# The tail behind an attention stream: gate, strip order, moved modes, transform places and last store, changed together

## The chip, the cores and the metric

The kernel runs on one core of one Trainium2 chip. The time is device time of one execution in microseconds (us), the median of the runs. A core has TensorE (PE: matmuls, with weight loads PEld beside them), VectorE (DVE), ScalarE (ACT), GpSimd (POOL) and SyncE (SP); each works through its own instructions in order, and they wait for one another by semaphores. SP, ACT and POOL issue DMA transfers, and all transfers of the core are moved by its 16 DMA engines. SBUF is the working memory with 128 partitions; PSUM is the memory that TensorE writes, eight banks of 2 KB a partition (512 fp32 numbers).

## The reference

Everything is fp32. The input x has shape (4, 64, 96, 96). Two layers follow one another, each applied to a group-normalised input (32 groups of two channels) and added to its own input:

```python
x = x + L0(gn(x))
x = x + L1(gn(x))
```

Layer 0 is attention over the N = 9216 pixels with a sigmoid in place of a softmax, and a channel gate:

```python
q, k, v = conv1x1(x, wq) + bq, conv1x1(x, wk) + bk, conv1x1(x, wv) + bv  # 8, 8 and 64 channels
out = V @ sigmoid(Q^T K)^T + x                                           # per image, 9216 x 9216
avg, mx = out.mean((2, 3)), out.max((2, 3))
mlp = lambda f: relu(f @ ca_w1.T) @ ca_w2.T
result = out * sigmoid(mlp(avg) + mlp(mx))[:, :, None, None]
```

Layer 1 is a spectral convolution. A real 2-D Fourier transform is taken of each channel; only 16 modes along w and 32 along h (the first and the last 16) are kept; for each mode the 64 input channels are mixed into 64 output channels by a complex matrix; the other modes are zero, and the transform back gives the result.

## The kernel before, in words

**Layout.** An image lies in SBUF as 128 partitions by 4608 columns: channel by half of the image (`x1`, `xs[p]`). A strip is 768 columns (8 rows in each half), six to an image. A block is 512 columns of queries, nine to an image.

**The stream.** For four images, one after another, TensorE computes energies (line 551), ScalarE takes the sigmoid from PSUM to SBUF (572), and TensorE multiplies by the values and accumulates over all keys in one bank (589). At the end of each block VectorE adds the bank to the block and sums it (595) and takes its maximum (597). The order of TensorE, ScalarE and VectorE is written out by hand here (`manual_schedule`, lists of steps `together`, `alone`, `ends` by time step `t`); the layer-1 work of images 0 to 2 is worked in among it. Only the last image's second layer is left when the stream ends; that is the tail, from line 914.

**Gate.** `after(p)` (612) makes three steps. `means` reduces the nine maxima and nine sums of the blocks and joins the halves; `hidden` is two small products (629, 630) and two steps on VectorE (631, 632); `gates` is one product with two columns (636), a sum of the two (639) and a sigmoid (640). Ahead of these, three matmuls without a use (917, 918) are queued on TensorE behind the last attention product.

**Strips.** The last image becomes x1 = x * gate + old x. The old x has been read again into `again` during the stream. For strips not in `ADDED`, VectorE does this (`combine`, 177); for those in `ADDED`, ScalarE scales (990) and GpSimd issues a DMA that adds `again` to x1 in SBUF (991). `strip(s)` (993) then transposes the strip on VectorE (997) into a place `t0` to `t3`, squares and sums it on ScalarE (1002) and multiplies it on TensorE by the transform along w (1007); three strips go into each of two groups. Steps of the normalisation (`group_stats`, 134) come between. Each group is turned (1014) and multiplied along h (1019), the result is turned again (1049) and scaled into `u` (1051, 1054). This part is again in a hand-written order for TensorE, ScalarE and VectorE; the rest of the tail is ordered by the compiler's scheduler. Weights of the modes are loaded into whatever room has come free (936): four rows once the stream ends, then into the strips' places and into `again`.

**Modes.** Eight steps q, each with two halves, mix four rows of modes with four matmul groups (215); the results go by turns through VectorE (130) and ScalarE (132) into `vms[q]`. They must change partitions for the transform back. For q up to 5, `keep` (224) stores them to DRAM (`vd`) in four DMAs and `back` (229) reads them in another order into `vt`: rows 0 to 15 by four DMAs of GpSimd behind q = 4, rows 16 to 23 by four of SP behind q = 5. For q = 6 and 7 TensorE moves them with selecting matrices into the PSUM tile `picked` (1096). Line 1100 adds `picked` to `vt`.

**Transform back and stores.** Two groups of products along h (1111) go into two PSUM tiles of two banks, four transposes (1117) into `z`. For each of six strips TensorE makes `py` (1127), in one of two PSUM places of two banks, VectorE adds it to x1 (1135) and a DMA stores it (`write`, 97), by turns from SP and ScalarE. Strip 0 goes in two halves.

`occupy` (961) queues matmuls without a use behind a given one.

## Time and profile before

| what | us |
|---|---|
| median of 3 runs (lowest, highest) | 3021.2 (3020.45, 3021.38) |
| profiled execution, whole | 3020.43 |
| its span, first to last instruction | 3018.7 |
| matmuls without a use begin behind the stream (918) | 2962.3 |
| gate (640) | 2965.8 |
| first transpose of a strip (997) | 2967.1 |
| mode products begin (215) | 2984.1 |
| add of moved modes (1100) | 3001.8 |
| first add of a last strip (1135) | 3007.2 |
| last add of a last strip begins (1135) | 3012.9 |
| TensorE busy | 3000.9 |
| ScalarE busy | 2406.6 |
| VectorE busy | 335.8 |

Times in the span count from its first instruction. A row of the timeline gives start, length, engine, line, operation, what it writes and reads, and in brackets how long the engine was idle before it and what the profile takes to have ended this. A row with x3 holds several instructions of the same kind, whose length then includes gaps. fp32 matmuls appear as two instructions each. "DMA to landing" is counted from an issue to the arrival of all its data. Where a wait is for several semaphores, the profile names one of them.

### The profile page before, as it was taken

The numbers are of one execution on the slowest core, as the hardware profiler recorded it, in microseconds if no ns is written. First come the engines' busy times: TensorE is split into PE (matmuls) and PEld (weight loads), VectorE is DVE, ScalarE is ACT, GpSimd is POOL, SyncE is SP. The second block draws the span as 40 slices with busy tenths as digits, with TensorE's granted clock in tenths as the row PEclk, the third lists the DMA queues.
The fourth block names the chain that finished last, engine by engine and source line by source line (L and its number), as shares of the span: only waits on it lengthen the run. The fifth ranks groups of instructions, "written<-read, shape, count | busy, mean of one in ns | idle before, by whom it ended". The sixth has DMA issues, their size and how long they took to land.

```text
span 3018.7 us, 44581 instructions
## 1 busy us (share of the span) xinstructions
PE 3000.9 (99%) x19360; PEld 1091.3 (36%) x19360; DVE 335.8 (11%) x814; ACT 2406.6 (80%) x1539; POOL 145.0 (5%) x295
## 2 busy tenths in 40 slices
PE   9999999999999999999999999999999999999998
PEld 3333333333333333333333333333333333333334
DVE  4100000002111000001311000000221110100104
ACT  5888888887887888888788888888788777777783
POOL 1100000004000000001300000000310000000000
PEclk9999999999999999999999999999999999999999
DMA  4000000002230000001322000000243243312224
GB/s 167 20 4 4 4 4 4 4 2 56 68 77 17 4 4 4 4 5 23 82 69 72 4 4 4 4 3 2 44 109 98 77 158 86 55 47 64 67 93 153
DMA packets 157267, 133.96 MB, mean 44 GB/s; under 512 B 118960, under 2 KB 123120, under 8 KB 156784
## 3 DMA queue, kind: packets, MB, share of 16 engines
q1 hardware_dynamic: 145152, 110.06, 13.5%
q0 software_dynamic: 11344, 19.69, 2.2%
q8 instruction: 152, 2.49, 0.3%
q10 hardware_dynamic: 576, 1.38, 0.1%
q14 instruction: 43, 0.35, 0.0%
HBM read 91.53 MB, written 38.73 MB: 43 GB/s over the span
## 4 chain that ended last, share of the span: by engine, by line
PE 98%; DVE 1%; DMA 0%; ACT 0%; issue 0%; SPq 0%; POOL 0%; DVEq 0%; ACTq 0%
PE banks L589 78%; PE banks L551 17%; PE banks L470 1%; PE banks L215 1%; PE banks L394 0%; PE pv L215 0%; PE banks L300 0%; PE banks L366 0%; DMA x<-in_x_dram 0%; PE banks L328 0%; ACT at L572 0%; PE pa L1007 0%; DVE xt L997 0%; PE banks L436 0%; DVE x L180 0%
## 5 line engine op out<-in xcount | busy, mean ns | idle before, releaser
L572 ACT ACTIVATE at<-banks 128x2048 f32<-128x2048 f32 (+1 forms) x1505 | 2388.9, 1638 | 548.2 <-PE banks L551 535.8
L589 PE MATMUL banks<-at,vT 128*64 128x512 f32 (+1 forms) x11780 | 2406.6, 548 | 0.0
L589 PEld LDWEIGHTS banks<-at,vT 128*64 128x64 f32 x11780 | 773.8, 136 | 1352.3 <-issue 1297.5
L551 PE MATMUL banks<-q,kT 32*128 32x512 f32 x5040 | 543.0, 452 | 0.3 <-ACT at L572 0.3
L551 PEld LDWEIGHTS banks<-q,kT 32*128 32x128 f32 x5040 | 223.6, 182 | 453.0 <-issue 331.4
L595 DVE SCALAR_TENSOR_TENSOR x<-banks,x 128x512 f32<-128x512 f32 x36 | 24.9, 692 | 1663.4 <-PE banks L589 1663.4
L521 POOL DMA_DIRECT2D stage<-qk x256 | 125.7, 499 | 937.7 <-DMA qk<-turned 927.1
L168 POOL TENSOR_TENSOR mr_l<-ve_l,cs 128x1 f32<-128x1 f32 x7 | 3.9, 556 | 1288.7 <-DVE ve_l L167 1288.7
L398 DVE TENSOR_TENSOR x<-banks,x 128x768 f32<-128x768 f32 x18 | 17.2, 958 | 212.3 <-PE banks L394 212.3
L470 PEld LDWEIGHTS banks<-cs,x 64*64 64x64 f32 x1152 | 22.6, 135 | 27.2 <-ACT at L572 25.6
L487 DVE TENSOR_TENSOR u<-banks,cs 128x128 f32<-128x128 f32 x35 | 10.2, 291 | 191.0 <-PE banks L470 191.0
L739 POOL DMA_DIRECT2D w_early<-in_spec_dram x12 | 6.4, 542 | 518.5 <-PE banks L394 357.7
L470 PE MATMUL banks<-cs,x 64*64 64x80 f32 (+1 forms) x1152 | 28.3, 236 | 0.0
L477 DVE TENSOR_TENSOR vT<-banks,cs 128x256 f32<-128x256 f32 x72 | 26.9, 415 | 0.0
L715 DVE COPY ae<-banks 128x512 f32<-128x512 f32 x9 | 6.2, 692 | 174.8 <-PE banks L300 128.8
L597 DVE TENSOR_REDUCE maxs<-x 128x1 f32<-128x512 f32 x36 | 24.7, 686 | 1.2
L715 DVE COPY ws<-banks 128x512 f32<-128x512 f32 x16 | 11.1, 692 | 116.8 <-PE banks L215 116.8
L603 DVE BATCH_NORM_STATS2 stats<-x 128x6 f32<-128x512 f32 x36 | 23.3, 681 | 4.3 <-DMA x<-in_x_dram 4.3
L180 DVE SCALAR_TENSOR_TENSOR x<-x,gate,old 128x768 f32<-128x768 f32 x18 | 18.2, 1009 | 17.5 <-DMA old<-in_x_dram 17.5
L508 DVE STREAM_TRANSPOSE turned<-t 128x384 f32<-128x384 f32 (+1 forms) x35 | 19.9, 568 | 1.4 <-DVE t L506 0.3
L551 PE MATMUL banks<-q_first,kT 32*128 32x512 f32 x144 | 16.6, 463 | 2.7 <-ACT at L572 1.8
L523 DVE CAST kT<-stage 128x256 fp32r<-128x256 f32 x64 | 16.0, 287 | 24.3 <-DMA stage<-qk 24.1
(144 smaller groups left out, 402.0 us busy)
## 6 DMA issues: line engine op xcount, KB each, us to landing
ws<-in_spec_dram SPq DMA_DIRECT2D x32, 512.0 KB
q<-qk SPq DMA_DIRECT2D x280, 32.0 KB
stage<-qk POOLq DMA_DIRECT2D x256, 32.0 KB, 1.9
out_dram<-x SPq DMA_DIRECT2D x20, 384.0 KB
x<-in_x_dram SPq DMA_DIRECT2D x9, 768.0 KB
old<-in_x_dram SPq DMA_DIRECT2D x18, 384.0 KB
x1d<-x SPq DMA_DIRECT2D x18, 384.0 KB
xd<-old SPq DMA_DIRECT2D x18, 384.0 KB
```

The costliest lines, as they stand in the source:

```text
L180: nc.vector.scalar_tensor_tensor(xs[p][:, cols], xs[p][:, cols], gate, old, ALU.mult, ALU.add)
L215: self.last = nc.tensor.matmul(pv[bass.ts(g, 32), :].rearrange("q (n k o) -> q n k o", n=SIDE, o=C)[:, :, k, :], self.ut[:, at:at + 32], s ...
L470: projected[0] = nc.tensor.matmul(pp[bass.ts(e, P // 2), b, 2 * a + h, :width], src[rows, a, h, bass.ts(e, P // 2)], named("wv")[rows, :wi ...
L477: nc.vector.tensor_tensor(vTs[p % 2][:, 8 * s:8 * s + 8, :].rearrange("p (a h b) m -> p b a h m", h=2, b=2)[:, b], pp[:, b, :, :C].rearran ...
L508: nc.vector.transpose(turned[:, k:].rearrange("p k a (m h) -> p (k a) h m", h=2), t[:, k:].rearrange("p k a h m -> p (k a) h m").bitcast(F32))
L521: nc.gpsimd.dma_start(come[bass.ts(r, QK), :], split[p][s // 2][:, r // 2, bass.ts(s % 2, NB // 2)])
L551: nc.tensor.matmul(banks[:, bank_of(i), :], kT[r:r + 32, i % TILES // 8, i // 4 % 2, :], ask[i // TILES][r:r + 32, :], start=True, stop=True)
L572: nc.scalar.activation(at[:, of:of + n, :], banks[:, bank:bank + n, :], AF.Sigmoid)
L589: attended[0] = nc.tensor.matmul(acc[half, cols], vTs[n // NBLK % 2][:, j, :], at[:, place(2 * pair + b), cols], start=(j == 0), stop=(j = ...
L595: nc.vector.scalar_tensor_tensor(blk, acc, 1.0, blk, ALU.mult, ALU.add, accum_out=sums[p][:, m:m + 1])
L597: mark[0] = nc.vector.tensor_reduce(maxs[p][:, m:m + 1], blk, AX.X, ALU.max)
L603: each = [lambda s=s: nc.vector.bn_stats(stats[:, s, :], xs[p][:, bass.ts(s, NB)]) for s in range(NBLK)]
```

## The change

Seven edits, all of the last image's tail or its preparation:

- `after_last` takes the place of `after` for the last image. Three sums and a maximum over what is known before the last block are taken in the last block of the stream (`known`). At the end of the last block, ScalarE sums the accumulator bank while writing it to a scratch place, and VectorE adds the bank to the block and takes the maximum in one instruction, starting from the known maximum. `means` has three steps in place of five, `hidden` one in place of two ahead of the next product, and the two columns are summed by accumulating in PSUM; the sigmoid reads PSUM.
- Strips go in the order 0, 1, 3, 2, 4, 5, and `ADDED` is (2, 5) in place of (4, 5). Places and steps between go by the position in this order.
- The stores of q = 5 are shared between SP and ScalarE; of the four reads of rows 16 to 23, SP issues two, GpSimd one, and ScalarE one, behind q = 7.
- `picked` has two banks, and its products are ordered by q first.
- The add of `picked` to `vt` is split in two halves of output channels.
- The two tiles of the transform along h and those of `py` share four places of two banks.
- The last strip's product, add and store go in two halves, as the first strip's do.

```diff
@@ -65,7 +65,8 @@
 SQ = 32
 NSQ = H // SQ
 NSTRIP = HALF // STRIP
-ADDED = (4, 5)
+ADDED = (2, 5)
+INTURN = (0, 1, 3, 2, 4, 5)
 APART, APART_LAST = 6, 4
 GN_EPS = 1e-5
 
@@ -221,9 +222,9 @@
             vm = self.vms[q].rearrange("q (n m) -> q n m", n=SIDE)
             self.move(vm[:, :, bass.ts(half, 2 * C)], pv.rearrange("q (n m) -> q n m", n=SIDE))
 
-        def keep(self, q, queue):
+        def keep(self, q, *queues):
             for g in range(4):
-                queue.dma_start(self.vd[4 * q + g],
+                queues[g % len(queues)].dma_start(self.vd[4 * q + g],
                                 self.vms[q][32 * g:32 * g + SIDE * 2 * self.n, :])
 
         def back(self, vt, to, first, rows, b, slot, n, parts, queue):
@@ -592,6 +593,13 @@
                 if j == NCH - 1 and cols.stop == NB:
                     p, m = divmod(n, NBLK)
                     blk = xs[p][:, bass.ts(m, NB)]
+                    if n + 1 == B * NBLK:
+                        nc.scalar.activation(at[:, 0, :], acc, AF.Identity,
+                                             accum_out=sums[p][:, m:m + 1])
+                        nc.vector.tensor_tensor_reduce(
+                            blk, acc, blk, 1.0, maxs[p][:, m - 1:m], ALU.add, ALU.max,
+                            accum_out=maxs[p][:, m:m + 1])
+                        continue
                     nc.vector.scalar_tensor_tensor(blk, acc, 1.0, blk, ALU.mult, ALU.add,
                                                    accum_out=sums[p][:, m:m + 1])
                     mark[0] = nc.vector.tensor_reduce(maxs[p][:, m:m + 1], blk, AX.X, ALU.max)
@@ -640,6 +648,48 @@
                 nc.scalar.activation(gate, gsum, AF.Sigmoid)
 
             return gate, [means, hidden, gates], f
+
+        def after_last(p):
+
+
+            f = small.tile([P, 2], F32, tag=f"f{p}", bufs=1, name=f"f_{p}")
+            fm = small.tile([P, 1], F32, tag="tot", name=f"fm_{p}")
+            top = small.tile([C, 1], F32, tag=f"top{p}", bufs=1, name=f"top_{p}")
+            hid = small.tile([R, 2], F32, tag=f"hid{p}", bufs=1, name=f"hid_{p}")
+            gate = small.tile([P, 1], F32, tag=f"gate{p}", bufs=1, name=f"gate_{p}")
+            last = NBLK - 1
+
+            def known():
+                rest = small.tile([P, 2], F32, tag="rest", bufs=1, name=f"rest_{p}")
+                nc.vector.tensor_reduce(rest[:, 0:1], sums[p][:, :last], AX.X, ALU.add)
+                nc.vector.tensor_reduce(rest[:, 1:2], xs[p][:, bass.ts(last, NB)], AX.X, ALU.add)
+                nc.vector.tensor_reduce(maxs[p][:, last - 1:last], maxs[p][:, :last], AX.X, ALU.max)
+                nc.vector.tensor_tensor(rest[:, 0:1], rest[:, 0:1], rest[:, 1:2], ALU.add)
+                known_sum.append(rest[:, 0:1])
+
+            known_sum = []
+
+            def means():
+                nc.vector.tensor_copy(top, maxs[p][C:, last:])
+                nc.vector.tensor_tensor(f[:C, 1:2], maxs[p][:C, last:], top, ALU.max)
+                nc.vector.tensor_scalar(fm, sums[p][:, last:], known_sum[0], 0.5 / HALF,
+                                        ALU.add, ALU.mult)
+
+            def hidden():
+                ph = bank_a(f"ph_{p}")
+                nc.tensor.matmul(ph[:R, 1:2], named("w1", C), f[:C, 1:2], start=True, stop=True)
+                nc.tensor.matmul(ph[:R, 0:1], named("w1"), fm, start=True, stop=True)
+                nc.vector.tensor_scalar(hid, ph[:R, 0:2], 0.0, None, ALU.max)
+                nc.vector.tensor_scalar(f[:, 0:1], fm, 2.0, None, ALU.mult)
+
+            def gates():
+                pg = bank_a(f"pg_{p}")
+                for i in range(2):
+                    projected[0] = nc.tensor.matmul(pg[:, 0:1], named("w2", R), hid[:, i:i + 1],
+                                                    start=(i == 0), stop=(i == 1))
+                nc.scalar.activation(gate, pg[:, 0:1], AF.Sigmoid)
+
+            return gate, [means, hidden, gates], f, known
 
         def warm(s, n=NB // 2):
 
@@ -779,6 +829,7 @@
             follow(None, lambda: fetch(1), 4)
 
         stats0 = {p: stats_of(p) for p in range(1, B)}
+        final = after_last(B - 1)
         ask, asked, known, valued, normal, renewed = {0: q}, 1, 3, 1, 2, NBLK
         heads = [HEAD]
         sizes, total, order, done, block, edges = [5], [5], [[4, 5, 6, 3, 2]], [], [], set()
@@ -818,6 +869,8 @@
                 if p == B and 3 <= m < 6:
                     for s in (2 * m - 6, 2 * m - 5):
                         end(t + 2, lambda s=s: bring(s))
+                if p == B and m == NBLK - 1:
+                    end(t + 2, final[3])
                 if m == NBLK:
                     assert not chain, (n, t, len(chain))
                     second_layer(p - 1, t)
@@ -912,7 +965,7 @@
                         step()
                     put_off = []
         spare[0] = 7
-        gate, steps, f = after(B - 1)
+        gate, steps, f, _ = final
         with tc.issue_after(attended[0].ins):
             for n in (NB, NB, NB // 4):
                 nc.tensor.matmul(banks[:, 3, :n], cs[:, :P], cs[:, :n], start=True, stop=True)
@@ -993,7 +1046,7 @@
         def strip(s):
 
             cols = bass.ts(s, STRIP)
-            xt = place_of(f"t{s % 4}", f"xt_{s}")[:, :STRIP]
+            xt = place_of(f"t{INTURN.index(s) % 4}", f"xt_{s}")[:, :STRIP]
             nc.vector.transpose(xt, x1[:, cols])
             if s == 0:
                 nc.vector.scalar_tensor_tensor(mv[:, 0:1], f[:, 0:1], gate, stats0[p][2][:, 0:1],
@@ -1029,12 +1082,12 @@
         less_constant = small.tile([P, 1], F32, tag="const", name="less_constant")
 
         with tc.manual_schedule(engines=ENGINES):
-            for s in range(NSTRIP):
+            for i, s in enumerate(INTURN):
                 if s not in ADDED:
                     combine(p, s, gate, again[:, bass.ts(s, STRIP)])
                 strip(s)
-                if s in (1, 3):
-                    steps[s // 2]()
+                if i in (1, 3):
+                    steps[i // 2]()
             var = small.tile([P, 1], F32, tag="var", name="var")
             rows_turned(0)
             rows(0)
@@ -1075,36 +1128,45 @@
         for q in range(KH // 4):
             l1.mix(q, 0)
             l1.mix(q, 1)
-            if q <= last - NPICK:
+            if q < last - NPICK:
                 l1.keep(q, nc.sync)
+            if q == last - NPICK:
+                l1.keep(q, nc.sync, nc.scalar)
             if q == 3:
                 nc.gpsimd.memset(vt, 0.0)
-            for first, rows_of, behind, queue in ((0, 16, last - 3, nc.gpsimd),
-                                                  (16, 16 - 4 * NPICK, last - 2, nc.sync)):
+            for first, rows_of, behind, queues in (
+                    (0, 16, last - 3, [nc.gpsimd] * 4),
+                    (16, 16 - 4 * NPICK, last - 2, [nc.sync, nc.gpsimd, nc.sync, None]),
+                    (16, 16 - 4 * NPICK, last, [None, None, None, nc.scalar])):
                 if q == behind:
-                    for half in range(2):
-                        for slot in range(2):
-                            l1.back(vt, 64 * half + 32 * slot, first, rows_of, 0, slot,
-                                    2 * half, 2, queue)
-
-        picked = mix_bank.tile([P, NB], F32, tag="picked", bufs=1, name="picked")
+                    for i, queue in enumerate(queues):
+                        if queue is not None:
+                            l1.back(vt, 64 * (i // 2) + 32 * (i % 2), first, rows_of, 0, i % 2,
+                                    2 * (i // 2), 2, queue)
+
         M = KW // SIDE * C
-        for n in range(2):
-            for q in range(last - NPICK + 1, last + 1):
+        picked = mix_bank.tile([P, 2, NB], F32, tag="picked", bufs=1, name="picked")
+        for q in range(last - NPICK + 1, last + 1):
+            for n in range(2):
                 for half in range(2):
                     at = 4 * (last - q)
                     l1.last = nc.tensor.matmul(
-                        picked[bass.ts(half, C), bass.ts(n, M)],
+                        picked[bass.ts(half, C), n, :M],
                         picks[:, 2 * half + n, at:at + C], l1.vms[q][:, bass.ts(2 * half + n, M)],
                         start=(q == last - NPICK + 1), stop=(q == last))
-        nc.vector.tensor_tensor(vt, picked, vt, ALU.add)
+        for i in range(2):
+            to = vt.rearrange("q (n k o) -> q n k o", n=2, o=C)[..., bass.ts(i, C // 2)]
+            nc.vector.tensor_tensor(
+                to, picked[:, :, :M].rearrange("q n (k o) -> q n k o", o=C)[..., bass.ts(i, C // 2)],
+                to, ALU.add)
         occupy(1, l1.last, mix_bank.tile([P, NB], F32, tag="v", name="idle_v", bufs=6))
 
         banks.close()
-        pz_bank, py_bank = psum("ps_z"), psum("ps_y", 2)
+        y_bank = psum("ps_y", 4)
         z = tail.tile([P, C, SQ], F32, tag="z", name="z_last")
         for i in range(2):
-            pz = pz_bank.tile([P, 4, NB // 2], F32, tag=f"z{i}", name=f"pz_{i}")
+            pz = y_bank.tile([P, 2, NB], F32, tag="y", name=f"pz_{i}")
+            pz = pz.rearrange("q b (x m) -> q (b x) m", m=NB // 2)
             for e in range(2):
                 for half in range(2):
                     rows_of = bass.ts(half, 2 * KH)
@@ -1116,10 +1178,10 @@
                 cols = slice(i * C // 2 + n * C // 4, i * C // 2 + (n + 1) * C // 4)
                 nc.vector.transpose(z[:, cols, :], pz.rearrange(
                     "q x (k o) -> q o (x k)", o=C // 2)[:, bass.ts(n, C // 4), :])
-        occupy(2, moved[0], py_bank.tile([P, 2, NB], F32, tag="y", name="idle_y")[:, 0])
+        occupy(2, moved[0], y_bank.tile([P, 2, NB], F32, tag="y", name="idle_y")[:, 0])
         for s in range(NSTRIP):
-            for part in ([0], [1]) if s == 0 else ([0, 1],):
-                py = py_bank.tile([P, 2, NB], F32, tag="y", name=f"py_{s}_{part[0]}")
+            for part in ([0], [1]) if s in (0, NSTRIP - 1) else ([0, 1],):
+                py = y_bank.tile([P, 2, NB], F32, tag="y", name=f"py_{s}_{part[0]}")
                 for n, i in enumerate(part):
                     for r in range(2):
                         rows_of = bass.ts(r, C)
```

## The prediction

> **What bounds the kernel.** I read the page's chain first, then the table by stretches, then the timeline from 2962 us on, engine by engine. The chain and the two stretches (columns: length, then busy us and instruction count of TensorE, its weight loads, VectorE, ScalarE, GpSimd; clock; DMA share; GB/s):

> ```profile
> PE 98%; DVE 1%; DMA 0%; ACT 0%; issue 0%; SPq 0%; POOL 0%; DVEq 0%; ACTq 0%
> ...
> 0.00:2962.40 2962.40, 2955.03 (x18899) 1061.58 (x18899) 303.17 (x755) 2392.75 (x1514) 139.94 (x286) 1.00 0.15 41
> 2962.40:3018.70 56.30, 45.88 (x462) 29.73 (x462) 32.66 (x59) 13.86 (x25) 5.11 (x9) 0.97 0.64 205
> ```

> TensorE's attention stream holds 2962.4 us at full clock and is untouched, but for four VectorE instructions placed in its last block, where VectorE idles for 76.8 us before the row at line 595; they need some 0.15 + 0.69 + 0.16 + 0.15 us and delay nobody. So only the last 56.3 us can move, and there the order of waits decides, not a busy engine. All times below are on the clock of the span before. The sum is made against the profiled execution: span 3018.7 and 1.7 around it, 3020.4; the median of the runs, 3021.2, lies 0.8 above that, and I carry the difference over to the median.

> **Gate.** The handover from stream to tail (timeline: start, length, engine, line):

> ```profile
> 2962.32 2.21 PE L918 MATMUL banks<-cs 128*128 128x512 f32 x6
> ...
> 2962.44 0.69 DVE L595 SCALAR_TENSOR_TENSOR x<-banks,x 128x512 f32<-128x512 f32 x1 [76.76 <-PE banks L589]
> ...
> 2963.17 0.69 DVE L597 TENSOR_REDUCE maxs<-x 128x1 f32<-128x512 f32 x1
> ...
> 2964.33 0.15 DVE L624 TENSOR_TENSOR f<-f,top 64x1 f32<-64x1 f32 x1
> ...
> 2964.54 0.19 PE L629 MATMUL banks<-f,cs 64*4 64x1 f32 x2
> ...
> 2965.22 0.38 PE L636 MATMUL banks<-hid,cs 4*128 4x2 f32 x2 [0.38 <-DVE hid L632]
> 2965.64 0.16 DVE L639 TENSOR_REDUCE gsum<-banks 128x1 f32<-128x2 f32 x1 [0.47 <-PE banks L636]
> 2965.83 0.20 ACT L640 ACTIVATE gate<-gsum 128x1 f32<-128x1 f32 x1 [6.76 <-DVE gsum L639]
> ```

> The add (0.69) and the maximum (0.69) become a sum on ScalarE beside one fused add-and-maximum on VectorE. The nearest row for the first is the Identity of 128x512 at line 454, 0.69, plus an accumulator read of 0.19 that overlaps it by 0.1; no table load appears between that Identity and the sigmoids, so none is priced. The fused instruction has no row; its floor is line 595's 0.69 + 0.08, its ceiling both passes, 1.38; I take 0.77, as line 595 also reads the bank, adds, writes and accumulates. If both ran at once, VectorE would be through at 2963.2, and three small steps at the spacing of 0.11 to 0.18 would give f at 2963.65, 0.83 earlier than 2964.48. [...] Both read the accumulator's bank. No run here shows two engines on one bank. [...] It makes little odds: the fillers of line 918 sit ahead of the first gate product on TensorE and their last pass starts at about 2964.33 and lasts 0.11, so TensorE is free at 2964.44 either way. Gain there: 0.1. The two hidden steps become one: 0.07 off. The sum of the two columns moves into TensorE: a second pair of passes costs 0.12 (the spacing of lines 629 and 630) to 0.3 (weight loads of 0.18 each); I take 0.25, since the weights are 128 columns here; the reduction saves 0.16 + 0.03. Gate in sum: -0.1 - 0.07 + 0.25 - 0.19 = **-0.1** (ends -0.25 and +0.6, the latter if the fused instruction takes 1.38).

> **Strips.** Before, strips 4 and 5 got their old x by an accumulating DMA; now 2 and 5 do, in the order 0, 1, 3, 2, 4, 5. Counts stay: four combines, six transposes, two scalings.

> ```profile
> DMA to landing us min/median/max: 5.4/6.3/7.2
> ...
> 2967.31 1.79 POOL L991 DMA_DIRECT2D x<-again  x2 [76.39 <-DVE x L180]
> ...
> 2972.17 0.97 DVE L180 SCALAR_TENSOR_TENSOR x<-x,gate,again 128x768 f32<-128x768 f32 x1
> ...
> 2973.18 0.98 DVE L997 STREAM_TRANSPOSE xt<-x 128x768 f32<-128x768 f32 x1
> ...
> 2974.21 4.15 PE L1007 MATMUL pa<-xt,lc 128*128 128x256 f32 x18 [0.35 <-DVE mr_l_last L157]
> ...
> 2974.31 1.98 DVE L997 STREAM_TRANSPOSE xt<-x 128x768 f32<-128x768 f32 x2
> ```

> The first transfer, issued at 2967.31, lands 5.4 later, 2972.7; the second, issued at about 2968.1, 7.2 later, 2975.3. Before, the first was wanted at 2974.3, 1.6 after its landing. Now strip 3's transpose ends at 2972.24 and strip 2's follows at once; it finds its data at 2972.7 and VectorE, in order, waits 0.45. An earlier gate hardly helps, because until about 2969.5 the transfer shares the engines with the four 512 KB loads that the end of the stream releases (DMA share 0.90 to 1.1 from 2967 to 2974). What is queued behind: the mean's two steps, strip 4's combine and transpose, strip 5's transpose. Strip 2 is transposed by 2973.7, strip 4 by 2976.0, strip 5 by 2977.0, where before 5 ended at 2976.3. TensorE needs 1.38 a strip (4.15 / 3): strip 4 from 2976.1, strip 5 from 2977.45 to 2978.85, against 2978.36 before. Without the wait it would be 2978.35: the new order alone gains nothing, as TensorE's last strips follow VectorE. Everything to the mode products (2984.1 before) moves by +0.5, less the gate's 0.1: **+0.4**. Ends: -0.2 (no wait) and +1.0 (landing 0.6 later). Weight loads that wait for strip 2's square start some 2 us later; the last of the loads are in by 2986.5 or so and these rows are used from 2994.5, so 8 us cover them.

> **Moved modes.** Order: store of q = 5 to DRAM, read back, add.

> ```profile
> 2993.63 3.01 SPq L226 DMA_DIRECT2D vd<-w_early  x8
> ...
> 2995.85 2.10 POOL L237 DMA_DIRECT2D vt<-vd  x4 [9.25 <-DMA vd<-w_early]
> ...
> 2998.07 2.28 PE L1096 MATMUL picked<-w_early,lc 128*64 128x256 f32 x16
> 2998.20 0.59 ACT L132 COPY w_early<-pv 128x512 f32<-128x512 f32 x1 [1.14 <-PE pv L215]
> ...
> 2998.82 1.30 SPq L237 DMA_DIRECT2D vt<-vd  x4
> ...
> 3001.81 0.69 DVE L1100 TENSOR_TENSOR vt<-picked,vt 128x512 f32<-128x512 f32 x1 [3.75 <-PE idle_v L965]
> ```

> The wait of line 1100 names TensorE, but the picks end by 3000.4; what came last is the fourth read back, issued at 2999.8, in by 3001.8 (2.0). The stores of q = 5 go out at 2995.35 in four issues of 0.3 and the last, of 2996.3, is in at 2998.75 (2.4). With two on SP and two on ScalarE's queue the last issue is at 2995.7 and all are in at 2998.1. ScalarE pays 2 x 0.34 in a gap of 1.13 before its copy at 2996.47: covered, with 0.45 to spare. Reads back: SP's two are issued by 2998.45, in at 3000.5; GpSimd's fifth waits 2998.1, starts some 0.5 later (its first four started 0.65 after their last wait passed) and lands 2.2 on, 3000.8; ScalarE's goes after its last copy, 2998.82 + 2.0 = 3000.85. The picks, now ordered by q, wait less for that copy and end near 3000. Add at 3000.9: -0.9 (ends -0.2, if one of the other queues is as late as SP was, and -1.2). The add is in halves of about 0.41 (the 128x256 row of line 477), so the first transform can start at 3001.3 where it started at 3002.55: **-1.2** in all. That needs the halves, interleaved in memory, to be told apart; the two engines writing u interleaved at 2982.8 at the same time show that this is done. If not, -0.8.

> **Last transforms and stores.**

> ```profile
> 3007.25 1.02 DVE L1135 TENSOR_TENSOR x<-py,x 128x384 f32<-128x384 f32 x2 [0.84 <-PE py L1127]
> ...
> 3008.86 1.82 DVE L1135 TENSOR_TENSOR x<-py,x 128x768 f32<-128x768 f32 x2 [0.59 <-PE py L1127]
> ```

> With two places the product of strip 1 waits for the first half's add, hence the 0.59. With four it starts 0.35 sooner, and the later waits of 0.19 go: strip 1's add ends 2.2 after the first add's start, not 2.57. From there stores bind: at 3011 to 3015 DMA is at 0.96 to 1.04 of its share with 364 to 393 GB/s, 1.03 us a strip, so five strips take 5.2 whatever VectorE does. So **-0.4**; the halved last store costs 2 x 0.55 - 0.95 = 0.15 on VectorE, which is ahead of the stores by then, and saves nothing while they are backed up. Ends 0 and -0.8.

> **Sum.** +0.4 - 1.2 - 0.4 = -1.2, gate included: span 3017.5, profiled time 3019.2, median **3020.0 us**.

> **Rivals.** (1) My own: strip 2 waits about 0.5, the rest gains; 3020.0, chance 0.50. (2) Strip 2 comes in time: -0.2 - 1.2 - 0.5 = -1.9, up to -2.4 with the larger ends; about 3019.0. For it: the issue may profit from the gate; against it: the shared DMA engines. 0.25. (3) The moved modes gain nothing, the wait only changing queue to GpSimd or ScalarE: +0.4 - 0.3 (the halved add alone) - 0.4 = -0.3, so 3020.9. For it: GpSimd's 0.65 before an issue and its landings of up to 2.6. 0.15. (4) Slower: strip 2 lands with strip 5, at 2975.3, because the two accumulating transfers and the weight load issued at 2970.4 share the DMA engines packet by packet. VectorE then waits 3.1, the mode products move by +3.0, and the end by 3.0 - 1.6 = +1.4: 3022.6. It decides from a landing of about 2973.9, 1.2 after the one shown. Against it: before, the first landed 2.6 ahead of the second. 0.10.

> **Range.** The lowest ends give -2.4 and the runs' scatter 0.5: 3018.2. Above, rival 3 with a wait of 1.0 gives +0.3 and scatter 0.5, 3022.0; this leaves part of rival 4 and the extremes out. Rivals 1 to 3 end on one side, so the one range serves. 0.2% of this time, about what a measurement of this kernel can tell from no change, is 6.0 us: no case reaches it. Same 0.95; 0.02 for faster and 0.03 for slower are left for what no row shows, such as a clock loss in the tail (the clock is 1.00 in every us up to 3015).

> **What would show it.** Right: the add of line 1100's successor starting 0.9 earlier relative to the mode products, the last adds without gaps over 0.2, strip 2's transpose waiting on its DMA, gate within 0.25 of before. Wrong: ScalarE and VectorE on the accumulator together; strip 2 without a wait; the stores ending more than 0.6 earlier after the first add; any change before 2962.

## The result, and the profile after

The changed kernel takes 3024.47 us (median of 20 runs, 3023.28 to 3026.64) where the kernel before takes 3020.43 beside it: 1.0013 times as long, 95% interval 1.0007 to 1.0019. That is within the 0.2% that the forecast called no change, but it is 4.0 us longer where 1.2 us less was predicted, and outside the range. The profiled execution has a span of 3023.5, 4.8 more than before.

First the page's chain, then the two stretches (columns as in the prediction):

```profile
PE 95%; issue 3%; DMA 1%; DVE 0%; ACT 0%; POOL 0%; SPq 0%; DVEq 0%; POOLq 0%; ACTq 0%
```

```profile
0.00:2962.40 2962.40, 2955.31 (x18898) 1061.12 (x18898) 303.71 (x759) 2392.56 (x1514) 140.12 (x286) 1.00 0.14 41
2962.40:3023.50 61.10, 47.60 (x466) 32.02 (x464) 31.78 (x57) 14.52 (x27) 5.66 (x10) 0.93 0.60 189
```

The stream is as before. The tail is 61.1 long instead of 56.3, its mean clock is 0.93 instead of 0.97, and TensorE is busy 1.7 longer in it although it has hardly more to do. The time at which the tail begins scatters between executions, from 2960.7 to 2964.2 in the profiles of this study, so from here on each stage is measured inside the tail. The table has them for all kernels. "Tail" runs from the first of the matmuls without a use (918 before) to the last instruction; "gate" to the start of the sigmoid; "strips" on to the first mode product; "modes" on to the first add of `picked` to `vt`; "back" on to the first add of a last strip; "adds" is the length of these adds; "end" is from the first of them to the last instruction. Spans are given to 0.1 us, so "end" and "tail" are good to 0.05. Each row is one profiled execution. e6 and e10 are one kernel profiled twice, and differ by 0.1 in the strips and by 0.7 in the end.

| kernel | gate | strips | modes | back | adds | end | tail |
|---|---|---|---|---|---|---|---|
| before | 3.51 | 18.29 | 17.69 | 5.44 | 6.60 | 11.45 | 56.38 |
| after | 3.45 | 18.64 | 20.90 | 7.90 | 5.46 | 10.20 | 61.09 |
| e1 | 3.45 | 18.53 | 17.48 | 5.17 | 5.45 | 10.14 | 54.77 |
| e3 | 3.52 | 18.29 | 21.12 | 8.24 | 6.60 | 11.40 | 62.57 |
| e4 | 3.45 | 19.18 | 20.90 | 5.17 | 5.45 | 10.25 | 58.95 |
| e5 | 3.45 | 18.44 | 17.34 | 5.18 | 5.45 | 10.18 | 54.59 |
| e6 | 3.44 | 18.26 | 17.44 | 5.17 | 5.46 | 10.82 | 55.13 |
| e7 | 3.45 | 18.57 | 17.38 | 5.17 | 5.39 | 10.64 | 55.21 |
| e8 | 3.45 | 18.73 | 17.35 | 5.18 | 6.74 | 11.48 | 56.19 |
| e9 | 3.45 | 18.86 | 17.06 | 5.17 | 5.46 | 10.60 | 55.14 |
| e10 | 3.45 | 18.35 | 17.46 | 5.18 | 5.45 | 10.11 | 54.55 |
| e11 | 3.51 | 18.30 | 17.92 | 5.17 | 5.45 | 10.95 | 55.85 |

After less before: gate -0.06, strips +0.35, modes +3.21, back +2.46, end -1.25; in sum +4.7. So two stages lose 5.7, and the rest gains 1.0. Both losing stages have a mark of their own in the profile.

**The modes: SyncE stands still.** SP's own waits, 2985 to 3006 us, in the kernel after (what is waited for, total us, times, longest):

```profile
SPq L227 <- DMA vd<-w_early: 5.0, 1, 5.0
SPq L227 <- DVE vm L131: 3.6, 1, 3.6
SPq L227 <- ACT vm L133: 1.7, 4, 0.7
SPq L238 <- DMA vd<-w_early: 1.4, 5, 0.4
```

and in the kernel before:

```profile
SPq L226 <- DVE vm L130: 3.6, 1, 3.6
SPq L226 <- ACT vm L132: 1.7, 4, 0.7
SPq L237 <- DMA vd<-w_early: 1.6, 3, 0.7
SPq L226 <- ACT w_early L132: 0.6, 2, 0.3
```

The first line after has no counterpart before. In `keep` (line 227), whose DMAs only wait for the copies that fill `vms[q]`, SP waits 5.0 us for another store, one of q = 5. The timelines say which (SP's in the kernel before, then those of SP, ScalarE and GpSimd in the kernel after):

```profile
2986.74 6.46 SPq L226 DMA_DIRECT2D vd<-vm  x16
```

```profile
2987.11 11.39 SPq L227 DMA_DIRECT2D vd<-vm  x16
2998.67 2.06 SPq L227 DMA_DIRECT2D vd<-w_early  x6
3002.51 0.61 SPq L238 DMA_DIRECT2D vt<-vd  x2
```

```profile
2995.75 0.86 ACTq L227 DMA_DIRECT2D vd<-w_early  x2
```

```profile
3001.05 2.68 POOL L238 DMA_DIRECT2D vt<-vd  x5 [14.08 <-DMA vd<-w_early]
```

The sixteen stores of q = 0 to 3 took SP 6.46 us before and take 11.39 now. SP's second store of q = 3 goes out at 2997.56, when ScalarE's first store of q = 5, issued at 2995.75, is done. The chain in order of time names that store, 1.80 from its issue to its landing, and shows what it drags along (start, length, engine, line):

```profile
2995.75 1.80 DMA vd<-w_early
...
2997.56 0.26 SPq L227
...
2999.32 1.74 DMA vd<-w_early
3001.05 1.38 POOL vt L238 x3
...
3003.17 1.96 DMA vt<-vd
...
3005.40 0.44 DVE vt L1159
3005.84 0.04 issue
3005.88 3.96 PE pz L1173 x16
3009.84 2.85 PE idle_y L1018 x4
3012.70 0.58 PE py L1189 x8
```

Behind the waiting store stand two more of q = 3, four of q = 4 and SP's two of q = 5; GpSimd's reads need the last store of q = 4 and start at 3001.05, where they started at 2995.85; the add starts at 3005.40, where it started at 3001.81.

**The way back: the clock.** TensorE before (two rows) and after (four rows; start, length, in brackets the idle time), and then the clock after in stretches (the last three columns are granted clock, DMA share, GB/s):

```profile
3002.55 2.17 PE L1111 MATMUL pz<-vt,lc 64*128 64x256 f32 x16 [1.14 <-DVE vt L1100]
3004.66 1.99 PE L965 MATMUL idle_y<-cs 128*128 128x512 f32 x4
```

```profile
3000.33 1.13 PE L1018 MATMUL idle_v<-cs 128*128 128x512 f32 x2
3005.88 3.96 PE L1173 MATMUL pz<-vt,lc 64*128 64x256 f32 x16 [4.43 <-DVE vt L1159]
3009.77 2.92 PE L1018 MATMUL idle_y<-cs 128*128 128x512 f32 x4
3012.63 4.18 PE L1189 MATMUL py<-lc,z_last 64*64 64x192 f32 x96
```

```profile
3002.00:3004.00 2.00, 0.00 (x0) 0.00 (x0) 0.00 (x0) 0.00 (x0) 1.72 (x4) 1.00 0.30 79
3004.80:3005.00 0.20, 0.00 (x0) 0.00 (x0) 0.00 (x0) 0.00 (x0) 0.00 (x0) 0.68 0.00 0
3006.00:3008.00 2.00, 2.00 (x10) 2.00 (x12) 0.16 (x1) 0.00 (x0) 0.00 (x0) 0.50 0.00 0
3011.60:3011.80 0.20, 0.20 (x2) 0.16 (x1) 0.00 (x0) 0.00 (x0) 0.00 (x0) 0.76 0.00 0
3012.00:3014.00 2.00, 2.00 (x34) 1.38 (x36) 0.70 (x2) 0.00 (x0) 0.00 (x0) 1.00 0.00 0
```

TensorE has nothing to do from 3001.46 to 3005.88. At 3004.87 (0.68 of full speed in that fifth of a us is 36% of it at 1.00 and the rest at 0.50) the granted clock falls to one half, and it is full again at 3011.70. The products along h therefore take 3.96 where they take 2.17 at full clock (the first row, and that of e4 below), and the fillers `idle_y` 2.92 where they take 1.98 (e4): 2.73 together. `py` waits in TensorE's queue behind these fillers, so this all ends on the way to the end.

### The profile page after: what moved, and what is told of

The parts are those of the page before. It is cut to its first block, busy times and chain, and to the rows that moved or that the text cites. A ratio compares the mean times of both kernels' runs of the same rounds, so it can differ in the third digit from the quotient of the medians.

```text
span 3023.5 us, 44602 instructions
## 1 busy us (share of the span) xinstructions
PE 3002.9 (99%) x19362; PEld 1093.1 (36%) x19362; DVE 335.5 (11%) x816; ACT 2407.1 (80%) x1541; POOL 145.8 (5%) x296
## 4 chain that ended last, share of the span: by engine, by line
PE 95%; issue 3%; DMA 1%; DVE 0%; ACT 0%; POOL 0%; SPq 0%; DVEq 0%; POOLq 0%; ACTq 0%
PE banks L590 75%; PE banks L552 16%; PE banks L471 1%; PE banks L216 1%; PE banks L395 0%; PE pv L216 0%; PE banks L301 0%; DMA w_early<-in_spec_dram 0%; PE banks L697 0%; PE banks L367 0%; PE banks L329 0%; DMA x<-again 0%; DVE x L1197 0%; DMA x<-in_x_dram 0%; ACT at L573 0%
## 5 line engine op out<-in xcount | busy, mean ns | idle before, releaser
L488 DVE TENSOR_TENSOR u<-banks,cs 128x128 f32<-128x128 f32 x35 | 10.2, 290 | 191.8 <-PE banks L471 191.8
```

## The experiments

The theory was: a store of ScalarE holds back SP, the add comes some 3 us late, and the clock falls because of the idle time. The first rival was that the reads over three queues, the order of `picked` or the strips' order delay the add. A second was that the loss in the way back is the four shared PSUM places, with the clock only a sign of it.

**e3: the kernel before, with two of the four stores of q = 5 on ScalarE's queue and no other part of the change** (`keep` takes several queues, as in the change).

```diff
...
-            if q <= last - NPICK:
+            if q < last - NPICK:
                 l1.keep(q, nc.sync)
+            if q == last - NPICK:
+                l1.keep(q, nc.sync, nc.scalar)
```

> The kernel before with one edit: two of the four stores of q = 5 go from ScalarE's queue. Theory A: SP stands for some 5 us in its stores of q = 3, the add of the picked modes starts near 3005.2 in place of 3001.8, TensorE idles over 4 us and its clock falls to a half for some us; time near 3026, 6 over before. Theory B: about +1. Theory C: no change, or 0.5 less than before.

Measured: 3026.81 (13 runs), 1.0019 times before, 1.0011 to 1.0027. Modes +3.43, back +2.80, all else as before: this one edit loses 6.4 us. SP's waits and TensorE's row:

```profile
SPq L226 <- DMA vd<-w_early: 5.0, 1, 5.0
```

```profile
3006.30 3.96 PE L1113 MATMUL pz<-vt,lc 64*128 64x256 f32 x16 [4.57 <-DVE vt L1102]
```

Here the two PSUM places of before are in use, and the clock falls all the same. So the reads, the strips and the four places are not needed for the loss.

**e1: the change, with the four stores of q = 5 on SP again.**

```diff
-            if q < last - NPICK:
+            if q <= last - NPICK:
                 l1.keep(q, nc.sync)
-            if q == last - NPICK:
-                l1.keep(q, nc.sync, nc.scalar)
```

> The changed kernel with all four stores of q = 5 on SP again; the four reads back stay on SP, GpSimd and ScalarE. Theory A (SP's stores of q = 3 are held behind a store of q = 5 on ScalarE's queue, because both use one of a few completion semaphores in rotation): SP sends its 24 stores without a wait for a DMA, their last lands near 2999.2, GpSimd's reads start near 2996.3, the add of the picked modes starts near 3001.9 (3005.4 in the changed kernel), TensorE's clock holds, and the time is some 6 us under the changed kernel, near 3018.4. Theory B (transfers spread over more queues land later, whichever they are): the add gains at most 1, time near 3023. Theory C (the time went to the gate or the strips): no change, 3024.5.

Measured: modes 17.48 and back 5.17; both losses are gone, and the tail is 54.77, 1.6 shorter than before. The median of 13 runs is 3021.02 (0.9999, 0.9991 to 1.0007), which does not show these 1.6; its runs spread from 3018.65 to 3023.65. About 3018.4 was expected, and what makes this median higher than that of e5 is open.

**Which wait it is.** Line 227 has no reason in the data to wait for a store of q = 5. The records of the traces name the semaphore on which each DMA of SP and ScalarE reports its landing: one of eight, in rotation. Before, each of the 800 DMAs of the two queues, in order of time, reports on the number that follows that of the one ahead of it; after, 792 of the 799 steps do, and the breaks lie at these stores and at the reads behind them. Nor does a DMA go out in these traces before the previous one on its number has landed: each trace has 792 such pairs, without an exception. The numbers follow the order of the compiled program and not that of time, as the list below and e5 show. The semaphore on which each store waits and then reports (numbered 0 to 7; from the two compiled programs, and the records of the two traces have the same numbers):

```
after  SP  q=0: 5 6 7 0  q=1: 1 2 3 5  q=2: 7 0 1 2  q=3: 3 4 5 6  q=4: 7 0 1 2  q=5: 3 4   ScalarE  q=5: 4 6
e5     SP  q=0: 5 6 7 0  q=1: 1 2 3 4  q=2: 5 6 7 0  q=3: 1 2 3 4  q=4: 5 6 7 0  q=5: 1 3   ScalarE  q=5: 2 4
```

In the kernel after, ScalarE's stores got their turn behind SP's third and fourth store of q = 1 (numbers 4 and 6 are missing there), though they have to wait for the copies of q = 5. SP's next user of number 4 is the second store of q = 3.

**e5: the change, with ScalarE's stores taking their turn behind SP's.** The same transfers from the same queues; the added dependencies only set the order in which the compiler takes the instructions, and no engine waits for them.

```diff
-                queues[g % len(queues)].dma_start(self.vd[4 * q + g],
-                                self.vms[q][32 * g:32 * g + SIDE * 2 * self.n, :])
+                sent = queues[g % len(queues)].dma_start(
+                    self.vd[4 * q + g], self.vms[q][32 * g:32 * g + SIDE * 2 * self.n, :])
+                if queues[g % len(queues)] is nc.sync:
+                    self.sent = sent
+                else:
+                    tc.add_manual_dep(sent.ins, self.sent.ins.name, mybir.DependencyInfo(
+                        mybir.DependencyClass.NoSync, mybir.DependencyReason.DATA),
+                        reason="lane")
+                    self.aside = sent
...
+            if q > last - NPICK:
+                tc.add_manual_dep(moved[1].ins, l1.aside.ins.name, mybir.DependencyInfo(
+                    mybir.DependencyClass.NoSync, mybir.DependencyReason.DATA), reason="lane")
```

> The changed kernel with every transfer on its queue and in its place on that queue; only the compiler's turn is fixed, so that ScalarE's two stores take their completion semaphores after SP's stores of q = 4, not between those of q = 1 and 2. Theory A: SP waits for no DMA, the stores of q = 5 have all landed near 2998.6, the add starts near 3001.3, time near 3017.8, at least 6 under the changed kernel. Theory B: as the changed kernel, the add near 3005, time 3024.

Measured: 3018.91 (13 runs; 0.9996, 0.9988 to 1.0004), which is 5.6 under the changed kernel where at least 6 was expected; modes 17.34, back 5.18, tail 54.59. SP's waits and timeline:

```profile
SPq L227 <- DVE vm L131: 3.6, 1, 3.6
SPq L245 <- DMA vd<-w_early: 2.2, 5, 0.7
SPq L227 <- ACT vm L133: 1.7, 4, 0.7
SPq L227 <- ACT w_early L133: 0.6, 2, 0.3
```

```profile
2988.71 6.46 SPq L227 DMA_DIRECT2D vd<-vm  x16
2995.61 2.33 SPq L227 DMA_DIRECT2D vd<-w_early  x6
3000.60 0.61 SPq L245 DMA_DIRECT2D vt<-vd  x2
```

No store waits for a store, and the sixteen take 6.46 as before. ScalarE issues its first store 11.24 after the first mode product, in the kernel after 11.25: the added dependencies held nothing up. So it was the turn at the semaphores, not the second queue as such. What the second queue saves is small: the modes take 17.34 against 17.48 with one queue (e1). In the kernel after, the same move cost 3.2.

**e4: the change, with twelve fillers `idle_v` in place of two**, so that TensorE is busy until the add and the add is as late as in the change.

```diff
-        occupy(1, l1.last, mix_bank.tile([P, NB], F32, tag="v", name="idle_v", bufs=6))
+        occupy(6, l1.last, mix_bank.tile([P, NB], F32, tag="v", name="idle_v", bufs=6))
```

> The changed kernel with six matmuls without a use behind the picks in place of one, so that TensorE is at work until about 3005.5. Theory A with a loss of clock as its second half: the add stays at 3005.4, the clock stays at 1.00 through the last transforms, their 16 matmuls take about 2.2 and not 3.96, and the first add of a last strip comes some 2.6 sooner after the add of the picked modes (7.9 in the changed kernel, 5.4 before); time near 3021.9. Rival (the last transforms are slower because of their four places and the halved add): no change, 3024.5.

Measured: 3022.75 (13 runs; 1.0007, 0.9998 to 1.0015). TensorE:

```profile
2999.40 5.42 PE L1018 MATMUL idle_v<-cs 128*128 128x512 f32 x12
3004.96 2.17 PE L1173 MATMUL pz<-vt,lc 64*128 64x256 f32 x16
3007.06 1.98 PE L1018 MATMUL idle_y<-cs 128*128 128x512 f32 x4
3008.98 4.18 PE L1189 MATMUL py<-lc,z_last 64*64 64x192 f32 x96
```

Modes stay at 20.90, back falls from 7.90 to 5.17. The whole loss of the way back, 2.73, is the clock, and the four places have no part in it. In this profile the strips took 19.18, 0.5 more than in the change (see below), so its tail is 2.1 shorter and not 2.7; the median is 1.7 below that of the change, where 2.6 was expected.

**e6 and e10: e5 with the strips in their old order** (the same kernel, run twice).

```diff
-ADDED = (2, 5)
-INTURN = (0, 1, 3, 2, 4, 5)
+ADDED = (4, 5)
+INTURN = (0, 1, 2, 3, 4, 5)
```

> The previous kernel with the semaphores in turn, and the strips in the order 0 to 5 with strips 4 and 5 added by DMA, as in the kernel before. If strip 2's wait for its accumulating DMA is all that the new order brings: no wait of VectorE for a DMA at strip 2, gate to mode products 18.29 (18.44 in the run with the new order, 18.29 in the kernel before), span and time 0.15 less. If the order also feeds TensorE better, the products come later than 18.44.

> The kernel with the semaphores in turn and the old order of strips, unchanged, in more rounds, since it is the fastest so far. If what the traces show adds up (gate -0.06, add of the picked modes -0.25, transforms -0.27, last strips -0.6 to -1.3), it is 1.2 to 1.9 under the kernel before, ratio 0.9994 to 0.9996, and 6 under the changed kernel; first mode product 18.26 after the gate again. If its first reading was luck, the ratio is 1.0000.

Measured: strips 18.26 and 18.35, before 18.29; with the new order they took 18.44 to 19.18 in the six profiles of after, e1, e4, e5, e7 and e8, where strip 2 waited 0.22 to 0.97 for its transfer each time. The new order costs 0.1 to 0.9 there and gains nothing. Times: 3018.40 (12 runs; 0.9993, 0.9984 to 1.0001) and 3018.26 (13 runs; 0.9991, 0.9982 to 0.9999). The interval of e10 is the only one of the study that lies below one, and only just; that of e6, the same kernel, does not. So a gain of 0.1% on the kernel before is likely, not certain. Its median stands 6.2 us below the changed kernel's, which was taken on another occasion. Against e5 (3018.91) the times alone do not tell; the strips' rows do.

**e9: e6, with GpSimd's single read of rows 16 to 23 given to ScalarE.**

```diff
-                    (16, 16 - 4 * NPICK, last - 2, [nc.sync, nc.gpsimd, nc.sync, None]),
-                    (16, 16 - 4 * NPICK, last, [None, None, None, nc.scalar])):
+                    (16, 16 - 4 * NPICK, last - 2, [nc.sync, None, nc.sync, None]),
+                    (16, 16 - 4 * NPICK, last, [None, nc.scalar, None, nc.scalar])):
```

> The kernel with the semaphores in turn and the old order of strips, and GpSimd's fifth read given to ScalarE, behind its last copy. If GpSimd's read is the last to land (it starts 0.6 after the two of SP): the add of the picked modes comes 16.9 after the first mode product, 0.4 sooner than with it (17.34), and the time is about 2.2 under the kernel before. If the stores' landing alone sets it: no change from 17.34.

Measured: modes 17.06, the shortest of all, 0.38 less than e6. In the trace of e6 GpSimd's fifth read is in 17.16 after the first mode product, the other three at 16.58 at the latest, and the add starts at 17.44; in e9 the last of the four is in at 16.82. So GpSimd's fifth read was the last one in. The time, 3019.47 (13 runs; 0.9995, 0.9987 to 1.0003), is no better than e6's; 2.2 under the kernel before was expected, and it is 1.0. In its profile the strips took 18.86 in spite of the old order, since strip 5 had to wait for its transfer:

```profile
2974.61 0.98 DVE L1057 STREAM_TRANSPOSE xt<-x 128x768 f32<-128x768 f32 x1 [1.08 <-DMA x<-again]
```

The landings of the accumulating transfers vary between executions: in the six profiles with the new order the faster of the two is in 5.1 to 5.9 us after its issue, the slower 6.6 to 7.5. With the old order only a late second one is felt, in three of the six profiles (0.18 in e3, 0.27 in e11, 1.08 in e9); with the new one the first is felt every time (0.22 to 0.97).

**e8: e5 with the PSUM places of before** (two for the products along h, two for `py`).

```diff
-        y_bank = psum("ps_y", 4)
+        pz_bank, y_bank = psum("ps_z"), psum("ps_y", 2)
...
-            pz = y_bank.tile([P, 2, NB], F32, tag="y", name=f"pz_{i}")
-            pz = pz.rearrange("q b (x m) -> q (b x) m", m=NB // 2)
+            pz = pz_bank.tile([P, 4, NB // 2], F32, tag=f"z{i}", name=f"pz_{i}")
```

> The kernel with the semaphores in turn, and with two PSUM places for the last strips' products, the transforms along h in a pool of their own, as before. Theory of the prediction (stores bind whatever VectorE does): the end comes 0.4 later after the first add, 10.6 in place of 10.2. Rival (the adds' spacing sets the end): the adds take 6.7 in place of 5.45 and the end is at 11.4 after the first add, 1.2 later.

Measured: 3019.92 (12 runs; 0.9997, 0.9989 to 1.0006). VectorE in e8, then in e5:

```profile
3006.82 1.02 DVE L1206 TENSOR_TENSOR x<-py,x 128x384 f32<-128x384 f32 x2 [0.84 <-PE py L1198]
3008.43 1.82 DVE L1206 TENSOR_TENSOR x<-py,x 128x768 f32<-128x768 f32 x2 [0.59 <-PE py L1198]
3010.44 2.29 DVE L1206 TENSOR_TENSOR x<-py,x 128x768 f32<-128x768 f32 x3 [0.19 <-PE py L1198]
3013.00 0.56 DVE L1206 TENSOR_TENSOR x<-py,x 128x384 f32<-128x384 f32 x1 [0.27 <-PE py L1198]
```

```profile
3008.62 5.45 DVE L1207 TENSOR_TENSOR x<-py,x 128x384 f32<-128x384 f32 x8 [0.84 <-PE py L1199]
```

The waits of 0.59 and 0.19 are back, the adds take 6.74 against 5.45, and the end 11.48 against 10.18. These are the figures of the rival, 6.7 and 11.4, and not of the theory. The table shows why: the end less the adds is 4.7 to 4.85 in eight of the twelve profiles, with two places as with four, and 5.1 to 5.5 in the other four (e6, e7, e9 and e11, all with four). So the end follows the last add, and "stores bind ... whatever VectorE does" does not hold. The bulk of the stores' data is through about 8.0 us after the first add with four places and 8.5 to 8.6 with two; it does not set the end, for in e4, with four places, it is through at 8.7 and the end is 10.25 all the same. As the last landing scatters by 0.8, one profile of e8 puts the worth of the four places between 0.5 and 1.4.

**e7: e5 with the last strip whole.**

```diff
-            for part in ([0], [1]) if s in (0, NSTRIP - 1) else ([0, 1],):
+            for part in ([0], [1]) if s == 0 else ([0, 1],):
```

> The kernel with the semaphores in turn, and the last strip's product, add and store whole. Theory of the prediction (stores are backed up by then): the end comes as long after the first add of a last strip as with halves, 10.2, within 0.15. Rival (the last store's own size is on the path): 0.3 to 0.5 later, about half of the 1.0 that a strip's store takes.

Measured: 3019.24 (12 runs; 0.9995, 0.9987 to 1.0004), end 10.64 against 10.18 in e5. e6, with halves, had 10.82, and the bulk of the data ended at the same 8.0. This experiment does not tell whether the halves bring anything; if so, it is less than the scatter of the landing, 0.8.

**e11: e6 with the old gate** (`after` for the last image too, its sum, add and maximum as in the other blocks).

```diff
-                    if n + 1 == B * NBLK:
+                    if False:
...
-        final = after_last(B - 1)
...
-                if p == B and m == NBLK - 1:
-                    end(t + 2, final[3])
...
-        gate, steps, f, _ = final
+        gate, steps, f = after(B - 1)
```

> The same kernel with the gate's steps as in the kernel before. The gate comes 3.51 after the first filler in place of 3.45, the rest as in the run beside it: 0.06 more in the trace and nothing that the times can tell. If the second read of the accumulator were free of the first, or the new gate cost the stream something, the difference would be 0.5 or more either way.

Measured: gate 3.51 against 3.44 in e6; 3019.57 (13 runs; 0.9995, 0.9987 to 1.0003). The new gate is worth 0.07, far below what the time can show. The rest was not as in e6: the modes took 17.92 instead of 17.44. SP's waits from 2980 to 3004 us have a line here that they do not have in e6:

```profile
SPq L227 <- DMA w_a<-in_spec_dram: 1.7, 2, 1.0
```

Two stores of SP wait for its own loads of weights (`w_a`), with which they share no data but the semaphore: each load stands eight places ahead of the store in the rotation and is still under way when its number comes round again. So the coupling also acts within one queue. What made these loads late in this execution is open.

## Why the prediction was wrong

**The step that failed** is that on the moved modes: "With two on SP and two on ScalarE's queue the last issue is at 2995.7 and all are in at 2998.1", and "ScalarE pays 2 x 0.34 ... covered". It asked what stands behind the two moved stores in ScalarE's queue, and not what a DMA of SP would then have to wait for; it took two queues to be independent. They share eight semaphores, and one of the moved stores held the one that SP needed at 2992.56, 3.2 us before that store was even issued (2995.75). In place of -0.9 the stage measured +3.21. The worst end given, -0.2, came from a queue "as late as SP was"; a wait of SP in a store that the change does not touch was in no rival. Rival 3 came nearest, in that a wait takes the place of the one removed, but put it on GpSimd or ScalarE and let it end at zero.

**The second loss followed from the first.** The step on the way back was right in its own terms: with the clock at full speed the halved add makes it 5.17 instead of 5.44, -0.27 for -0.3. What it put at nothing is the clock: a loss was left among the 0.03 of the chances "for what no row shows", though an add 3 us later leaves TensorE idle for 4.4. In the kernel after the clock falls at 3004.87, is full again at 3011.70, and falls once more behind the last matmul, at 3021.94: 6.83 and 10.24 apart, two and three times 3.41. In the 3.41 us before the first fall TensorE had no matmul, in the 3.41 behind it TensorE was busy for 2.40, and only in the next 3.41 for all of it. In e3 the fall comes 3.71 after the last matmul and the return again 6.83 later, with 2.56 busy in the first 3.41 behind the fall. What sets the moment of a fall or of a return these runs do not show. Nor had TensorE been idle throughout before every fall: in e8, at the end, the clock falls at 3014.35, behind 3.41 us in which TensorE was busy for 1.52, and in the kernel after 1.70 busy of 3.41 (3015.11 to 3018.52) left it full. A fall at the end costs nothing, since no matmul follows.

**What held.** With the semaphores in turn (e5) the change comes near the sum: tail -1.8 where -1.2 was predicted; the median, 3018.9 against 3020.4 beside it, has an interval that includes no gain. That the sums are so near is partly luck, since the moved modes brought less than half of what was reckoned and the end three times as much. In the parts:

- Gate: -0.06 for -0.1, near by luck: the first product starts no earlier (2.26 after the first filler instead of 2.22, where 0.1 earlier was reckoned), and from there to the sigmoid it is 1.19 instead of 1.29, where 0.01 less was reckoned. ScalarE and VectorE did not work on the accumulator together, which the forecast had named as a mark against itself: VectorE's fused instruction begins 0.72 after ScalarE's reading of the same bank and 0.03 after ScalarE's accumulator read ends at 2963.27, and its row names ScalarE (VectorE's timeline, after; the second row is strip 2's transpose):

```profile
2963.30 0.75 DVE L599 CUSTOM_DVE_ANT_0 x<-banks,x,maxs 128x512 f32<-128x512 f32 x1 [76.70 <-ACT at L597]
...
2972.66 0.98 DVE L1050 STREAM_TRANSPOSE xt<-x 128x768 f32<-128x768 f32 x1 [0.43 <-DMA x<-again]
```

- Fused instruction: 0.75 and 0.08 for reading its maximum, which overlap by 0.07, priced at 0.77.
- Strips: +0.35 for +0.5; strip 2 waits 0.43 (second row above) for the 0.45 predicted. Over the profiles with the new order the wait ran from 0.2 to 1.0.
- Moved modes, once in turn: -0.35 for -0.9. The stores of q = 5 are in some 14.5 after the first mode product instead of 14.0, and GpSimd's fifth read is the last one; without it -0.6 (e9).
- End: -1.25 for -0.4, beyond the larger end given, -0.8. The waits that were to go did go, and the adds take 5.46, where 6.2 was reckoned with. The term that held the gain down, stores that bind "whatever VectorE does", was wrong (e8): in the fourth us after the first add the stores moved 227 GB/s before and 384 after, so before they were still waiting for adds. The end follows the last add, by 4.85 before and by 4.74 after, so nearly all of the gain is that the adds are 1.14 shorter.

## What to carry to other kernels

When a DMA is given to another engine's queue, ask not only what stands behind it there, but which earlier DMAs it can hold back: look in the compiled program for the semaphore that it takes and for the next DMA that needs the same one. A DMA that waits for a DMA with which it shares no data is the mark of this in the profile, and putting the moved one in its turn cured it here without giving up the move. A DMA that comes late can still hold one behind it on the same semaphore (e11, 1.7 us for two stores). And where a delay leaves TensorE idle for some microseconds, add to the delay what half speed costs: here 1.1 us of idle time cost nothing (before), and 4.4 and 4.6 us cost 2.7 and 2.8 us more. A few fillers that fill the gap are the cheap insurance (e4: back 5.17 in place of 7.90).
